# Moving output stores and residual rows from SyncE's DMA queue to GpSimd's in the second half of a quantized feed-forward

## Chip, cores and metric

One core of a Trainium2 chip runs the whole kernel in one launch. The metric is the device time of an execution in microseconds (us). The engines are TensorE (PE: matmuls; its weight loads are PEld), VectorE (DVE), ScalarE (ACT), GpSimd (POOL) and SyncE (SP). SP does no arithmetic: it issues DMAs. POOL can issue DMAs too.

## What is computed

Two batches of 2048 tokens of width 512 pass through four residual steps: a cross attention, a block that works on 256 selected tokens of each batch, a second cross attention, and a feed-forward with quantized activations and ternary weights. Only the last matters here:

```python
def bit_linear(x, w):          # act_quant: 8-bit integers per token, weight_quant: -1, 0, 1
    return einsum('bsd,hd->bsh', act_quant(x), weight_quant(w))
h = bit_linear(layernorm(x), w1)              # 512 -> 2048
h = silu(depthwise_conv1d(h, conv_w, conv_b)) # three taps along the tokens
x = x + tanh(g_ffn[1]) * bit_linear(h, w2)    # 2048 -> 512
```

`act_quant` needs the largest magnitude over a token's 2048 inner values before any of them can be rounded, so the step falls into a first half (up to `silu`) and a second half (rounding, the product with `w2`, the residual).

## The kernel before

The 4096 tokens are 8 blocks (g = 0 to 7) of 512. A block's inner values lie as 16 groups of 128 channels by 512 tokens.

**First half, block by block** (`first_half` L1179, `convolved` L1154). For each of the 16 channel groups, four matmuls (L1159) fill a PSUM tile `ph`. VectorE scales it into `u` (L1169). Two columns at the left of `u` come from `carry`, the last two tokens of the block before, copied by POOL (L1168), and POOL saves the new last two columns (L1170). ScalarE and VectorE apply the three taps (L1171, L1175). Four groups at a time go through Silu (L1200), are stored to DRAM as `h_d` (L1206), and then are overwritten in place by their magnitudes (L1207), so that instruction waits for the store. For the last block (g = LAST = 7) nothing is stored; the values stay in SBUF. The convolution makes a row tile begin one token before its block, so the first row tile of each batch has 127 rows, and each batch's very last token is left over for `last_tokens`.

**Rounding.** Blocks 0 to 3 (EARLY) are rounded to integers while the second attention still runs, and wait in DRAM as `hq_d`. Blocks 4 to 7 are rounded in the second half itself by `quantize_hidden` (L1334): it loads an inner row group from `h_d` into a pool of eight buffers, six ahead (L1355), multiplies by the scale on VectorE (L1364) and rounds on VectorE (L1370) or ScalarE (L1367, L1368). Blocks 0 to 3 are loaded ready-made (L1348).

**Second half** (the loop at L1430). For each of a block's four row tiles of 128 tokens, `down_and_out` (L1384) runs 16 matmuls of the integers with `w2q` (L1388) into one of four PSUM tiles, VectorE scales and adds the residual row tile (L1391), and the result is stored to the output (L1392). `row_tile` (L1311) loads the residual rows (L1318, L1320) about four row tiles ahead, into eight `x5` buffers (and two `x5w` buffers for the first two), so that a load waits for the store that last used its buffer. `last_tokens` (L1394) handles the two leftover tokens: Silu, largest magnitude, two transposes, scale, rounding, then two one-row `down_and_out` calls of 16 matmuls each. It is called whole ahead of block 6.

**What sets the order.** The functions are generators advanced by hand, which interleaves the blocks' steps with the attention and with each other. The layer that records them arranges each engine's instructions by its own estimate of their times. After that each engine works strictly in its order. A DMA-issuing instruction waits in its engine's order until the data and the buffer are free, and all that stands behind it on that engine waits too. In the program before, all DMAs of this stage are issued on SP: integers, inner-row stores and loads, residual rows and output stores, mixed.

Of the kernel before, what the change touches and what calls it, by code (L numbers as in the profile page):

```python
# [17 lines left out]
P = 128  # L18
# [3 lines left out]
BLK = 512  # L22
TB = BLK // P
NBLK = S // BLK
# [19 lines left out]
def flamingo_kernel(ctx: ExitStack, tc: tile.TileContext, a: dict, out: bass.AP):  # L44
    nc = tc.nc
# [699 lines left out]
    with ExitStack() as st:  # L745
# [16 lines left out]
            out=pick,  # L762
            in_=pick,
# [10 lines left out]
            out=after,  # L774
            in_=after,
# [310 lines left out]
    LAST = B * NBLK - 1  # L1086
    EARLY = 4
    hq_d = [dramp.tile([P, HC, BLK], BF16, name=f"hq_d{g}") for g in range(EARLY)]
    x3_d = [dramp.tile([S, D], F32, name=f"x3_d{b}") for b in range(B)]
# [64 lines left out]
    def convolved(g, c, z):  # L1154

        cr = carry[g // NBLK]
        ph = ps_mm.tile([P, BLK], F32, name="ph", tag="mm")
        for d in range(DC):
            nc.tensor.matmul(  # L1159
                ph,  # L1160
                w1q[:, d, ts(c, P)],
                xiT[g][:, d, :],
                start=(d == 0),
                stop=(d == DC - 1),
            )

        u = act4.tile([P, BLK + 2], F32, name="u", tag="u", bufs=3)
        nc.gpsimd.tensor_copy(u[:, 0:2], cr[:, c, :])  # L1168
        nc.vector.tensor_tensor(u[:, 2:], ph, inv_b[g], ALU.mult)  # L1169
        nc.gpsimd.tensor_copy(cr[:, c, :], u[:, BLK:])  # L1170
        nc.scalar.activation(  # L1171
            z, u[:, 1 : BLK + 1], AF.Identity, scale=cw[:, c, 1:2], bias=cb[:, c : c + 1]
        )
        for k in (0, 2):
            nc.vector.scalar_tensor_tensor(  # L1175
                z, u[:, ds(k, BLK)], cw[:, c, k : k + 1], z, ALU.mult, ALU.add
            )
# [96 lines left out]
    def beside4(u, share=2):  # L1274


        for _ in range(share):
            advance(ending)
            advance(stream)
        if u is None or u % 4 != 1:  # L1280
            advance(later)
# [29 lines left out]
    def row_tile(g, i):  # L1311

        t = w5[0].tile([P, D], F32, name="x5w", tag="x5w", bufs=2)
        if g * TB + i > 1:
            t = act5[0].tile([P, D], F32, name="x5", tag="x5", bufs=8)
        r, p = g % NBLK * BLK + i * P - 1, 0
        if r < 0:
            nc.sync.dma_start(out=t[0:1, :], in_=x3_d[g // NBLK][0:1, :])  # L1318
            r, p = 0, 1
        nc.sync.dma_start(out=t[p:, :], in_=x3_d[g // NBLK][ds(r, P - p), :])  # L1320
        return t, r, p

    def second_half_starts():
        units.close()
        w5.append(s4.enter_context(tc.tile_pool(name="w5", bufs=1)))
        w5.append(w5[0].tile([P, HC, D], BF16, name="w2q"))
        nc.sync.dma_start(out=w5[1], in_=w2_d)
        ps_5.append(psum_pool(s4, "s5_o", 4))
        quantizing.extend(quantize_hidden(g) for g in range(2))
        for q in quantizing:  # L1330
            next(q, None)
        ahead.extend(row_tile(0, i) for i in range(2))

    def quantize_hidden(g):  # L1334

        hq[g] = []

        def integer_tile():

            pool, bufs = (w5[0], 12) if next(next_integers) % 24 < 12 else (act5[0], 12)  # L1340
            hq[g].append(pool.tile([P, GQ, BLK], BF16, name="hq", tag="hq", bufs=bufs))
            return hq[g][-1]

        if g < EARLY:
            for k in range(HC // GQ):
                if g == 1 and k == HC // GQ // 2:
                    yield
                nc.sync.dma_start(out=integer_tile(), in_=hq_d[g][:, ts(k, GQ), :])  # L1348
            return

        def load(c):
            if g == LAST:
                return kept[c // GC][:, c % GC, :]
            h = xr.tile([P, D], F32, name="x3", tag="x3")
            nc.sync.dma_start(out=h, in_=h_d[g][:, c, :])  # L1355
            return h

        AHEAD = 6
        hs = [load(c) for c in range(AHEAD)]
        s_b = scales_spread(g)  # L1360
        yield
        for c in range(HC):
            h = hs.pop(0)
            nc.vector.tensor_tensor(h, h, s_b, ALU.mult)  # L1364
            q = (integer_tile() if c % GQ == 0 else hq[g][-1])[:, c % GQ, :]
            if c % 4:
                nc.scalar.activation(h, h, AF.Copy, bias=RND)  # L1367
                nc.scalar.activation(q, h, AF.Copy, bias=-RND)  # L1368
            else:
                nc.vector.tensor_scalar(q, h, RND, RND, ALU.add, ALU.subtract)  # L1370
            if c + AHEAD < HC:
                hs.append(load(c + AHEAD))
            if c % 2:
                yield
# [6 lines left out]
    act5.append(s4.enter_context(tc.tile_pool(name="act5", bufs=1)))  # L1381
    w2q = w5[1]

    def down_and_out(rows, col, n, t, to, p=0):  # L1384

        po = ps_5[0].tile([n, D], F32, name="po4", tag="o4")
        for c in range(HC):
            nc.tensor.matmul(  # L1388
                po, rows(c), w2q[:, c, :], start=(c == 0), stop=(c == HC - 1)
            )  # L1390
        nc.vector.scalar_tensor_tensor(t, po, col, t, ALU.mult, ALU.add)  # L1391
        nc.sync.dma_start(out=to, in_=t[p:, :])  # L1392

    def last_tokens():  # L1394

        h = act5[0].tile([P, B, HC], F32, name="hl", tag="hl")
        nc.scalar.activation(h, z_last, AF.Silu)
        own = row4.tile([P, B], F32, name="ownl", tag="lm")
        nc.vector.tensor_reduce(own, h, AX.X, ALU.max, apply_absolute_value=True)
        pm = ps_mm.tile([P, B, P], F32, name="pml", tag="mm")  # L1400
        for b in range(B):
            nc.tensor.transpose(pm[:, b, :], own[:, b : b + 1].to_broadcast([P, P]), ident)
        m = row4.tile([P, B], F32, name="ml", tag="lm")
        nc.vector.tensor_reduce(m, pm, AX.X, ALU.max)
        nc.vector.tensor_scalar(m, m, 1e-5, None, ALU.max)
        s = row4.tile([P, B], F32, name="sl", tag="ls")
        nc.vector.reciprocal(s, m)
        nc.vector.tensor_scalar(s, s, 127.0, None, ALU.mult)
        fin = row4.tile([P, B], F32, name="fl", tag="lf")
        nc.vector.reciprocal(fin, s)  # L1410
        nc.vector.tensor_scalar(fin, fin, finstep, None, ALU.mult)
        q = act5[0].tile([P, B, HC], BF16, name="ql", tag="ql")
        for b in range(B):
            nc.vector.tensor_scalar(h[:, b, :], h[:, b, :], s[:, b : b + 1], None, ALU.mult)
        nc.vector.tensor_scalar(q, h, RND, RND, ALU.add, ALU.subtract)
        for b in range(B):
            t = act5[0].tile([P, D], F32, name="x5", tag="x5", bufs=8)[0:1, :]
            nc.sync.dma_start(out=t, in_=x3_d[b][S - 1 : S, :])
            down_and_out(
                lambda c: q[:, b, c : c + 1],  # L1420
                fin[0:1, b : b + 1],
                1,
                t,
                out[(b + 1) * S - 1 : (b + 1) * S, :],
            )

    while later:
        advance(later)
    ahead.extend(row_tile(0, i) for i in range(2, TB))
    for g in range(LAST + 1):  # L1430
        if g == LAST - 1:
            while stream or ending:
                beside4(None)
            last_tokens()
        behind = quantizing[1] if g == 0 else quantize_hidden(g + 1) if g < LAST else iter(())
        for i in range(TB):
            t, r, p = ahead.pop(0)
            down_and_out(
                lambda c: hq[g][c // GQ][:, c % GQ, ts(i, P)],
                hid_f[:, g * TB + i : g * TB + i + 1],  # L1440
                P,
                t,
                out[ds(g // NBLK * S + r, P - p), :],
                p,
            )
            if g < LAST:
                ahead.append(row_tile(g + 1, i))
            for _ in range(3):
                next(behind, None)
                beside4(None, 1)  # L1450
# [65 lines left out]
```

## Time and profile before

| what | value |
|---|---|
| median of 3 runs | 1788.83 us (1788.56 to 1795.08) |
| the profiled execution, its own time | 1791.24 us |
| its span | 1789.2 us |
| mean granted TensorE clock | 0.966 |
| PE busy | 1647.3 us (92% of the span) |
| DVE busy | 1250.1 us (70%) |
| ACT busy | 1101.7 us (62%) |
| POOL busy | 536.0 us (30%) |
| hardware DMA queue of SP | 192.23 MB, 31.5% of 16 engines |
| GpSimd's software DMA queue | 2.10 MB, 0.6% |
| last attention block's projections end | about 1616 us |

Times inside the profile are us from the start of the span. "Granted clock" is the share of full speed that TensorE was given in a stretch. A wait row reads "who waited, at which line <- who ended it: total us, times, longest us". A timeline row gives start, duration, engine, line, operation and tiles; SPq rows are DMA issues on SP, and their duration is the time of the issue, not of the transfer. Digits of names are left out, so the tile `x` stands for `x3` and `x5` alike: `x<-h_d` is a load of inner rows (L1355), `x<-x_d` a load of residual rows, `out_x<-x` an output store.

### The profile page before, as it was taken

The page shows a single profiled execution, that of the slowest core. Times are in us where ns is not written, and L with a number is a line of the kernel's source. Part 1 is how long each engine was busy: PE and PEld are TensorE (multiplying, and loading weights), DVE is VectorE, ACT ScalarE, POOL GpSimd, SP SyncE. Part 2 cuts the span into 40 slices and gives each one's busy share as a digit, 9 for nine tenths or more (in the row PEclk, how much of TensorE's full clock was granted, in tenths as well). Part 3 has the DMA queues.
Part 4 walks back from the last instruction along what each step waited for, and adds up shares of the span by engine and source line. Part 5 has one row for each costly group of instructions (what it writes and reads, how often), then busy time and mean ns, then how long its engine had stood idle before and what let it go on. Part 6 is the DMA issues. An engine that isn't in the chain of part 4 may idle for free.

```text
span 1789.2 us, 25277 instructions
## 1 busy us (share of the span) xinstructions
PE 1647.3 (92%) x8122; PEld 864.8 (48%) x8122; DVE 1250.1 (70%) x2544; ACT 1101.7 (62%) x3170; POOL 536.0 (30%) x671
## 2 busy tenths in 40 slices
PE   6999889899999889999999999999999999889968
PEld 3544444455555665755444544445454544434423
DVE  4566878865767443344378789897998789686956
ACT  2876566456553233345367778787787778744555
POOL 2534443342440011033134242432424224231100
PEclk9999999999999999999999999999999999899979
DMA  6011011121007861630012333233242233157374
GB/s 215 7 66 55 35 60 66 59 65 54 25 36 250 287 190 64 190 83 25 19 53 95 127 122 117 91 130 110 94 167 76 87 105 130 62 210 249 123 233 173
DMA packets 119828, 196.99 MB, mean 110 GB/s; under 512 B 12900, under 2 KB 50532, under 8 KB 115984
## 3 DMA queue, kind: packets, MB, share of 16 engines
q1 hardware_dynamic: 117872, 192.23, 31.5%
q0 software_dynamic: 960, 2.10, 0.6%
q8 instruction: 64, 1.05, 0.2%
q10 hardware_dynamic: 864, 1.05, 0.2%
q14 instruction: 68, 0.56, 0.1%
HBM read 120.89 MB, written 74.45 MB: 109 GB/s over the span
## 4 chain that ended last, share of the span: by engine, by line
PE 29%; DVE 15%; DMA 5%; ACT 4%; issue 2%; POOL 1%; SPq 1%; DVEq 0%; POOLq 0%; ACTq 0%
PE pq L253 8%; PE pp L320 8%; DVE h L1175 4%; PE po L302 3%; PE ph L1159 3%; PE sc L276 3%; PE po L1388 2%; PE tp L294 2%; DMA x<-h_d 1%; DVE u L1169 1%; DVE AT L295 1%; DVE nmx L119 1%; DMA hq<-hq_d 1%; DVE hf L1258 1%; DMA h_d<-h 1%
## 5 line engine op out<-in xcount | busy, mean ns | idle before, releaser
L122 ACT ACTIVATE A<-sc,nmx 128x128 f32<-128x128 f32 x1024 | 363.8, 385 | 131.5 <-DVE nmx L119 121.7
L131 POOL TENSOR_TENSOR A<-A,rden 128x512 f32<-128x512 f32 x256 | 275.9, 1079 | 506.7 <-DVE rden L130 410.8
L320 PE MATMUL pp<-L_wo,OT 128*128 128x512 f32 x768 | 366.8, 609 | 18.0 <-DVE x L329 11.9
L253 PE MATMUL pq<-xnT,L_wq 128*128 128x512 f32 x768 | 345.7, 598 | 12.2 <-DVE x L329 12.2
L122 ACT ACTIVATION_READ_ACCUMULATOR A<-sc,nmx 128x1 f32 x1024 | 229.7, 224 | 0.0
L253 PEld LDWEIGHTS pq<-xnT,L_wq 128*128 128x128 f32 x768 | 142.8, 191 | 172.1 <-issue 151.3
L119 DVE TENSOR_REDUCE nmx<-sc 128x4 f32<-128x512 f32 x256 | 168.6, 678 | 71.8 <-PE sc L276 71.6
L320 PEld LDWEIGHTS pp<-L_wo,OT 128*128 128x128 f32 x768 | 136.5, 193 | 164.4 <-issue 133.2
L1175 DVE SCALAR_TENSOR_TENSOR h<-u,cw,h 128x512 f32<-128x512 f32 x256 | 205.0, 834 | 6.0 <-ACT h L1171 5.5
L294 PE MATMUL tp<-ident,A 128*128 128x128 f32 x1024 | 164.4, 284 | 18.7 <-POOL A L131 13.2
L294 PEld LDWEIGHTS tp<-ident,A 128*128 128x128 f32 x1024 | 118.4, 143 | 87.6 <-issue 41.9
L295 DVE COPY AT<-tp 128x512 f32<-128x512 f32 x192 | 129.8, 678 | 43.5 <-PE tp L294 42.8
L276 PEld LDWEIGHTS sc<-L_kT,qT 32*128 32x128 f32 (+1 forms) x2048 | 110.6, 192 | 71.0 <-issue 58.5
L1388 PE MATMUL po<-w2q,hq 128*128 128x512 bf16 x512 | 122.2, 394 | 20.0 <-DVE hq L1370 9.0
L276 PE MATMUL sc<-L_kT,qT 32*128 32x128 f32 (+1 forms) x2048 | 137.0, 293 | 3.8 <-ACT A L122 3.2
L1171 ACT ACTIVATE h<-u,cb,cw 128x512 f32<-128x512 f32 x128 | 99.1, 808 | 64.7 <-DVE u L1169 53.6
L302 PE MATMUL po<-AT,L_v 128*32 128x512 f32 (+1 forms) x512 | 119.3, 657 | 11.7 <-DVE AT L295 11.1
L1159 PE MATMUL ph<-xiT,w1q 128*128 128x512 bf16 x512 | 124.3, 379 | 1.9 <-DVE u L1169 1.5
L1169 DVE TENSOR_TENSOR u<-ph,inv_b 128x512 f32<-128x512 f32 x128 | 84.9, 682 | 31.4 <-PE ph L1159 27.3
L130 DVE RECIPROCAL rden<-den 128x4 f32<-128x4 f32 x256 | 43.3, 169 | 80.0 <-ACT A L122 72.8
L1168 POOL COPY u<-carry 128x2 f32<-128x2 f32 x128 | 48.7, 382 | 167.3 <-DVE h L1175 141.3
L1170 POOL COPY carry<-u 128x2 f32<-128x2 f32 x128 | 49.8, 394 | 150.9 <-DVE u L1169 149.1
(238 smaller groups left out, 2362.6 us busy)
## 6 DMA issues: line engine op xcount, KB each, us to landing
h_d<-h SPq DMA_DIRECT2D x28, 1024.0 KB, 4.1
x_d<-x SPq DMA_DIRECT2D x64, 256.0 KB, 3.1
hf<-h_d SPq DMA_DIRECT2D x64, 256.0 KB, 3.4
x<-x_d SPq DMA_DIRECT2D x61, 256.0 KB, 4.7
x<-h_d SPq DMA_DIRECT2D x48, 256.0 KB, 5.5
x_d<-xo SPq DMA_DIRECT2D x32, 256.0 KB, 2.1
xf<-x_d SPq DMA_DIRECT2D x32, 256.0 KB, 3.6
hq_d<-hi SPq DMA_DIRECT2D x64, 128.0 KB, 1.8
```

Source lines behind the costliest of these rows:

```text
L119: nc.vector.tensor_reduce(nmx, sc, AX.X, ALU.max, negate=True)
L122: nc.scalar.activation(out_tile[:, h, :], sc[:, h, :], AF.Exp, bias=nmx[:, h : h + 1], accum_out=den[:, h : h + 1],)
L131: nc.gpsimd.tensor_tensor(out_tile, out_tile, rden.unsqueeze(2).to_broadcast([P, n, width]), ALU.mult,)
L253: nc.tensor.matmul(pq, W.wq[:, d, ts(e, P)], xnT[:, d, :], start=(d == 0), stop=(d == DC - 1),)
L276: nc.tensor.matmul(sc[h][:, t, :], qT[e % cpg][r, ts(t, P)], W.kT[r, b, e, :], start=True, stop=True,)
L294: nc.tensor.transpose(tp[:, t, :], A[:, t, :], ident)
L295: copy(AT, tp.rearrange("p t n -> p (t n)"))
L302: nc.tensor.matmul(po[h * dh : (h + 1) * dh, :], W.v[:, b, ts(hd, dh)], AT[c * hpc + h], start=True, stop=True,)
L320: nc.tensor.matmul(pp, OT[e][:, ts(i, P)], W.wo[:, e, :], start=(e == 0), stop=(e == nE - 1),)
L1159: nc.tensor.matmul(ph, w1q[:, d, ts(c, P)], xiT[g][:, d, :], start=(d == 0), stop=(d == DC - 1),)
L1175: nc.vector.scalar_tensor_tensor(z, u[:, ds(k, BLK)], cw[:, c, k : k + 1], z, ALU.mult, ALU.add)
L1388: nc.tensor.matmul(po, rows(c), w2q[:, c, :], start=(c == 0), stop=(c == HC - 1))
```

## The change

In the second half, residual-row loads (L1318, L1320) and output stores (L1392) are issued on GpSimd's queue; only block 7's output stores stay on SP. Block 7's carry copies (L1168, L1170) go from GpSimd to VectorE. `last_tokens` becomes a generator that is advanced once after each row tile of blocks 6 and 7, so that its transposes, its scale and rounding, and its two products come after row tiles 0, 1 and 3 of block 6; the products then stand between blocks 6 and 7. Its own residual loads stay on SP, its output stores go to GpSimd's queue.

```diff
-        nc.gpsimd.tensor_copy(u[:, 0:2], cr[:, c, :])
+        carried = nc.vector if g == LAST else nc.gpsimd
+        carried.tensor_copy(u[:, 0:2], cr[:, c, :])
         nc.vector.tensor_tensor(u[:, 2:], ph, inv_b[g], ALU.mult)
-        nc.gpsimd.tensor_copy(cr[:, c, :], u[:, BLK:])
+        carried.tensor_copy(cr[:, c, :], u[:, BLK:])
...
         if r < 0:
-            nc.sync.dma_start(out=t[0:1, :], in_=x3_d[g // NBLK][0:1, :])
+            nc.gpsimd.dma_start(out=t[0:1, :], in_=x3_d[g // NBLK][0:1, :])
             r, p = 0, 1
-        nc.sync.dma_start(out=t[p:, :], in_=x3_d[g // NBLK][ds(r, P - p), :])
+        nc.gpsimd.dma_start(out=t[p:, :], in_=x3_d[g // NBLK][ds(r, P - p), :])
...
-    def down_and_out(rows, col, n, t, to, p=0):
+    def down_and_out(rows, col, n, t, to, p=0, queue=nc.gpsimd):
...
-        nc.sync.dma_start(out=to, in_=t[p:, :])
+        queue.dma_start(out=to, in_=t[p:, :])
...
             nc.tensor.transpose(pm[:, b, :], own[:, b : b + 1].to_broadcast([P, P]), ident)
+        yield
...
         nc.vector.tensor_scalar(q, h, RND, RND, ALU.add, ALU.subtract)
+        yield
+        yield
         for b in range(B):
...
-            last_tokens()
+            last = last_tokens()
...
                 p,
+                nc.sync if g == LAST else nc.gpsimd,
             )
             if g < LAST:
                 ahead.append(row_tile(g + 1, i))
+            if g >= LAST - 1:
+                next(last, None)
```

## The prediction

> **What bounds the kernel now.** I first read the page's 40 slices. TensorE (PE) is busy in nearly all of them, and its dips come late, where the granted clock (PEclk) dips too. The change touches only the last stage, so I cut the end into stretches by what TensorE works on and read the engines' busy time in each:
>
> ```profile
> core 0: us, PE busy (x) PEld busy (x) DVE busy (x) ACT busy (x) POOL busy (x), PEclk, DMA share, GB/s
> 1569.00:1600.00 31.00, 29.71 (x89) 12.96 (x90) 29.26 (x40) 15.19 (x15) 15.86 (x27) 1.00 0.75 267
> 1600.00:1616.00 16.00, 9.97 (x22) 4.15 (x20) 10.53 (x17) 7.73 (x6) 1.43 (x4) 0.79 0.22 90
> 1616.00:1643.00 27.00, 22.97 (x108) 10.95 (x107) 13.62 (x28) 11.99 (x15) 1.20 (x2) 0.87 0.71 230
> 1643.00:1696.00 53.00, 51.63 (x244) 23.76 (x243) 49.01 (x82) 27.37 (x27) 12.13 (x29) 1.00 0.49 176
> 1696.00:1760.00 64.00, 46.77 (x195) 18.89 (x193) 42.23 (x83) 39.82 (x72) 0.00 (x0) 0.84 0.74 247
> 1760.00:1789.00 29.00, 24.77 (x111) 10.23 (x111) 17.91 (x30) 15.80 (x29) 0.00 (x0) 1.00 0.31 110
> ```
>
> TensorE stands still for 6.0 us in 1600–1616 (call it A), 4.0 in 1616–1643 (B), 1.4 in 1643–1696 (C), 17.2 in 1696–1760 (D) and 4.2 in the tail (E). A, B and D also run at a clock of 0.79 to 0.87. In C TensorE and VectorE (DVE) are both nearly full: block 7's first half and the down projections of blocks 0 to 3. Next, who waits for whom after 1600:
>
> ```profile
> DVE x L1364 <- DMA x<-h_d: 16.5, 7, 9.2
> ACT h L1207 <- DMA h_d<-h: 13.2, 3, 7.9
> PE po L1388 <- DVE hq L1370: 9.0, 2, 8.7
> ```
>
> Columns: total us, times, longest. Transfers end all three. The 7.9 us wait for an inner-row store is A (PE waits 6.03 us behind it), the 9.2 for an inner-row load is most of D. Why are they late? SyncE's (SP) own queue in D:
>
> ```profile
> 1719.05 0.26 SPq L1392 DMA_DIRECT2D out_x<-x  x1
> 1719.40 5.46 SPq L1355 DMA_DIRECT2D x<-h_d  x2
> 1724.95 0.53 SPq L1392 DMA_DIRECT2D out_x<-x  x1
> 1725.57 9.70 SPq L1355 DMA_DIRECT2D x<-h_d  x6
> ```
>
> An issue on SP normally takes 0.34 us. The store at 1719.05 is the 127-row one of block 4 (batch 1's first row tile). The two loads behind it take 5.46 us to issue, the next six 9.70, and that store lands 9.5 us after issue where the median is 2.0. The other 127-row transfers show the same: 1586.4 (the issue behind it 5.05 us), 1620.43 (7.88 us for two) and 1679.88 (lands after 12.3). Each inner-row transfer queued behind one is late: A follows 1586.4, B 1620.43, D 1719.05. And SP is held by what it waits for:
>
> ```profile
> SPq L1392 <- DVE x L1391: 42.6, 20, 8.0
> SPq L1320 <- DMA out_x<-x: 22.2, 12, 6.2
> ```
>
> The output stores wait for VectorE and the residual loads (buffers shared with those stores) for stores to land: 65 us in which the inner-row loads behind them can't go.
>
> **The change, part by part.** The profiled execution took 1791.24 us (span 1789.2, 2 us around it); the median of the runs is 1788.83, so I sum against 1791.24 and take 2.4 off.
>
> *Moved off SP:* 28 row-tile stores, 2 last-token stores and 34 residual-row DMAs, 64 issues, all four 127-row ones among them; on SP stay the 48 inner loads, block 7's four stores and the last tokens' two loads. In the changed program's order block 6's second inner store follows the 0.3 us integer loads directly, and each inner load waits only for its own buffer.
>
> *Stretch A.* In before the store could go when Silu ended at 1588.64, was issued at 1591.51 behind the 5.05 us, and landed at 1603.5. Alone it takes 4.1 us (the row `h_d<-h`), so about 1594; ScalarE (ACT) has other work to 1595.6. That removes 7.9 us of wait, TensorE's 6.0, and the half-speed matmuls after it (4 of 0.85 us in place of 0.43: 1.7). Against it: GpSimd (POOL) now issues three loads just ahead of the four bias adds (1571.48 in before) and the copies behind them. No POOL row shows this DMA; the nearest, the gather of 128 rows of 2 KB, takes 1.0 us (L970), the tiny one 0.6 (L66), the scatter 1.6 (L675). 3 x 1.0 = 3 us of delay to a copy that ScalarE waits for, perhaps 2 of it on the path (0 to 4.8). Sum: -7.7 + 2.2, so **-5.5**.
>
> *Stretch B.* The third inner store lands 7.9 us after issue with the 127-row store beside it; at 4.1 the fourth normalised tile, queued behind it on ACT, comes 3 us sooner. TensorE's transposes of the last block sit behind matmuls that wait for integer loads until 1636.93 (the 7.88 us issue); with loads early, the stretch from 1634.2 to the first matmul at 1642.3 shrinks from 8.1 us to about 4. POOL's rsqrt (L90) now stands behind four loads, 4 us from the moment the last projection ends, where statistics take 2 to 3 us anyway: cost 0 to 2, hidden mostly. Sum **-7**, at best -9, at worst -3.
>
> *Stretch C.* 32 carry copies move from POOL to VectorE, which is full (49.0 of 53). The nearest DVE rows:
>
> ```profile
> 1684.39 0.18 DVE L1219 TENSOR_TENSOR tap<-carry,cw 128x16 f32<-128x16 f32 x1
> 1684.49 0.17 DVE L1220 TENSOR_TENSOR z_last<-carry,cw 128x16 f32<-128x16 f32 x1
> ```
>
> Starts lie 0.10 us apart: 32 x 0.10 = 3.2 us; by duration 0.17 x 32 = 5.4. The handoff to POOL goes away (up to 2 back, and a gain of 1 isn't excluded). I take **+3** (-1 to +5.4).
>
> *Stretch D.* Now the loads start when the first buffers come free (1698–1699), not at 1703.24, and the 9.2 us hole behind 1719.05 closes. What is late next? The transfers themselves: 64 us x 247 GB/s = 15.8 MB. The best rates that this trace holds over 30 us and more are 267 (first row above) and 287 (page). At 280 the stretch needs 56 us, at 267 59, at 287 55. VectorE's 42, ACT's 40 and TensorE's 47 (about 40 at full clock) fit below that. So -8; the clock returns with the hole, **-9** in all (-4 to -17, the last if TensorE's idle went entirely).
>
> *Stretch E.* The last tokens' 32 matmuls (7.07 us at 1748.58) filled a hole; now they stand between blocks 6 and 7, where block 7's integers take VectorE and ACT 14 us after block 6's anyway while TensorE has some 20 matmuls left (4 us): 4 + 7 < 14, **0** (0 to +5 if those integers are early). Last stores stay on SP: 2.0 us to land.
>
> Sum: -5.5 - 7 + 3 - 9 = -18.5; 1791.2 - 18.5 - 2.4 = **1770**.
>
> **Two rules against the rows.** For 127 rows: the Trainium skill, "DMA: Bandwidth & Descriptors", section on why a DMA increments its semaphore by 16, says that a hardware-queue DMA over 127 partitions runs on one engine, and that GpSimd's queue spread 127 over all 16. The rows agree with the first half (9.5 us for 254 KB, 2.0 for 256); no run here shows the second. If it is false, the queued transfers still share that one engine, and A, B and D give half. Against the change speaks "SBUF — State Buffer", "Two separate sides", with its trap: GpSimd can't write descriptors while VectorE runs a two-port operation; a DMA of 620 ns became 3100. The gathers here took 0.95 to 1.09 us beside VectorE at work. At 1.0 us POOL needs 2 us per row tile for its store and load, plus up to 3.4 us where a load waits for the store before it; a row tile comes every 4.7 to 5 us on average. That fits. At 3.1 it would not. I take 1.0, since VectorE's stretches of such operations here are short (L1370, 0.42 us).
>
> **Rivals.**
> 1. *GpSimd's queue becomes the bound (slower).* About eight store-and-load pairs in a row each contain a landing wait (3.4 us at best for a gather). At 2.5 us per issue a pair takes 8.4 us: eight are 67 us where 55 are there, 12 late; then 20 tiles at 2 x 2.5 + 1.5 against 5.2 lose 26 more. 38 - 18.5 = +19: 1808. It decides from about 1.9 us per issue (2 x 1.9 + 1.5 = 5.3). For it: the rule, and the 1.6 us scatter. Against: 1.0 us gathers, and residual rows asked for eight tiles ahead.
> 2. *One engine keeps the 127 rows, or the transfers in D don't speed up:* A -2, B -3, C +3, D -4: about 1783.
> 3. *Copies at POOL's price* (0.39 each, L1170): C +12.5, sum -9: 1780.
> 4. *TensorE full:* idle of A, B and D (27) and half of their clock loss (4), less C's 3: -28, 1760.
>
> **How the numbers follow.** Forecast 0.45 (1763 to 1778), rival 4 0.17, rivals 2 and 3 together 0.22, rival 1 0.16 (some of it mild). About 0.5% (9 us) is what a measurement of this kernel can tell. Under 1780: 0.45 + 0.17 + 0.06 = 0.68. Within: 0.18. Slower: 0.14. Range 1756 to 1793.
>
> **What would show it.** A: the in-place magnitude (L1207 here) waits under 1 us for `h_d<-h`. B: no SP issue above 2 us near the block-0 stores. C: copies at 0.1 us pitch on DVE. D: DMA above 265 GB/s in its stretch, waits for `x<-h_d` under 8 us in total. POOL: its DMA issues near 1.0 us, 127-row ones landing in under 5. I am wrong if those issues take 2 us or more, or if the loads in D are no faster though nothing stands before them.

## The result and the profile after

The changed kernel took 1768.99 us (median of 4 runs, 1767.29 to 1771.65) beside 1788.69 before: ratio 0.9887, 95% interval 0.9863 to 0.9911. Taken once more later, beside other experiments, it gave 0.9908 (0.9892 to 0.9923). So it is about 1% faster; 1770 was predicted. The profiled execution took 1771.65 us, its span 1770.0.

The same stretches as before, by what TensorE works on; columns are time, then PE, PEld, DVE, ACT and POOL busy, granted clock, DMA share, GB/s:

```profile
1573.00:1604.00 31.00, 28.79 (x85) 12.53 (x88) 30.49 (x41) 18.55 (x17) 15.88 (x28) 1.00 0.77 271
1604.00:1614.00 10.00, 10.00 (x30) 4.29 (x29) 10.00 (x16) 4.79 (x5) 1.90 (x4) 1.00 0.33 134
1614.00:1637.00 23.00, 19.16 (x102) 9.37 (x103) 13.79 (x35) 11.89 (x16) 8.12 (x14) 1.00 0.96 355
1637.00:1688.00 51.00, 50.01 (x228) 22.71 (x232) 49.88 (x110) 26.59 (x25) 11.42 (x21) 1.00 0.44 150
1688.00:1739.00 51.00, 42.76 (x190) 17.22 (x193) 41.99 (x84) 40.85 (x74) 10.23 (x18) 1.00 0.89 305
1739.00:1770.00 31.00, 26.67 (x120) 10.94 (x120) 18.38 (x31) 14.74 (x27) 4.93 (x9) 0.98 0.28 100
```

A no longer has TensorE standing still (10.00 busy of 10.00), its clock is back at 1.00, and D fell to 51 us at 305 GB/s. The waits in the changed part after 1590:

```profile
POOL x L1321 <- DMA out_x<-x: 58.0, 17, 6.7
POOL out_x L1393 <- DVE x L1392: 33.0, 10, 7.1
...
DVE x L1365 <- DMA x<-h_d: 5.3, 6, 1.4
...
ACT h L1208 <- DMA h_d<-h: 3.5, 1, 3.5
```

The waits for stores and for VectorE now stand on POOL. The wait for inner-row loads fell from 16.5 us to 5.3, that of the in-place magnitude from 13.2 to 3.5. The four 127-row transfers, now on GpSimd's queue (last column: us from issue to landing):

```profile
x5w<-x_d POOLq DMA_DIRECT2D x1, 254.0 KB, 8.6
out_x<-x5w POOLq DMA_DIRECT2D x1, 254.0 KB, 8.1
x<-x_d POOLq DMA_DIRECT2D x1, 254.0 KB, 2.8
out_x<-x POOLq DMA_DIRECT2D x1, 254.0 KB, 4.2
```

Their 128-row neighbours on the same queue take 9.0, 8.7, 4.6 (the median of the loads) and 3.9: the 127 rows are no longer special. A GpSimd issue takes 0.55 us (0.50 to 0.78).

To compare kernels I use the end of the last product of attention weights with values (L302), just ahead of the first changed instruction, and these marks behind it: end of the last attention projection (A), first matmul of block 7's first half (B), end of the reduce that gives block 7's scale (C), end of block 6's last scaling on VectorE (D), end of the span (E). The part ahead of them is the same work in every kernel (VectorE, ScalarE and GpSimd run the same instructions there in the same order in all profiles), yet its end lay between 1569.0 and 1576.7 us. So medians that lie 3 or 4 us apart tell little here. The sum of the stretches, which leaves that part out, is the better measure, though it comes from one profile of each kernel; the changed kernel's two profiles differ by 2 us in it.

| kernel | median us | ratio (95% interval) | A | B | C | D | E | sum |
|---|---|---|---|---|---|---|---|---|
| before | 1788.7 | 1 | 47.4 | 25.9 | 53.7 | 63.9 | 29.4 | 220 |
| changed | 1769.0 | 0.9887 (0.9863-0.9911) | 41.0 | 20.7 | 53.6 | 50.4 | 31.3 | 197 |
| e11 changed again | 1774.9 | 0.9908 (0.9892-0.9923) | 41.0 | 22.4 | 53.6 | 50.1 | 32.2 | 199 |
| e1 before, 127 rows on GpSimd's queue | 1765.9 | 0.9874 (0.9858-0.9890) | 40.7 | 17.5 | 54.4 | 46.7 | 30.5 | 190 |
| e2 before, 127 cut 112 + 15 on SP | 1762.6 | 0.9858 (0.9839-0.9877) | 39.2 | 18.0 | 53.8 | 48.5 | 29.8 | 189 |
| e3 changed, 127 rows back on SP | 1804.0 | 1.0073 (1.0055-1.0091) | 50.7 | 32.3 | 54.5 | 58.6 | 32.4 | 229 |
| e4 changed, carry on GpSimd | 1775.2 | 0.9924 (0.9908-0.9940) | 41.0 | 22.5 | 53.8 | 49.4 | 32.2 | 199 |
| e5 e1 + carry on VectorE | 1762.5 | 0.9842 (0.9820-0.9864) | 40.7 | 17.5 | 53.6 | 47.2 | 30.5 | 190 |
| e6 e1 + last tokens in pieces | 1767.2 | 0.9871 (0.9849-0.9893) | 40.7 | 17.5 | 54.3 | 46.4 | 31.2 | 190 |
| e7 changed, 128-row stores on SP | 1771.8 | 0.9893 (0.9866-0.9919) | 41.0 | 22.4 | 53.6 | 47.3 | 32.5 | 197 |
| e8 changed, 128-row loads on SP | 1765.3 | 0.9865 (0.9844-0.9885) | 41.4 | 18.0 | 54.3 | 46.9 | 32.3 | 193 |
| e9 before, 127 cut 122 + 5 on SP | 1768.4 | 0.9890 (0.9869-0.9910) | 39.2 | 18.8 | 53.8 | 53.7 | 29.6 | 195 |
| e10 e2 + carry on VectorE | 1764.4 | 0.9838 (0.9818-0.9859) | 39.2 | 18.0 | 53.6 | 49.1 | 30.1 | 190 |

### The profile page after: what moved, and what is told of

It is laid out like the page before. It is cut to its first block, busy times and chain, and to the rows that moved or that the text cites. A ratio compares the mean times of both kernels' runs of the same rounds, so it can differ in the third digit from the quotient of the medians.

```text
span 1770.0 us, 25204 instructions
## 1 busy us (share of the span) xinstructions
PE 1642.2 (93%) x8076; PEld 863.0 (49%) x8122; DVE 1251.5 (71%) x2576; ACT 1101.4 (62%) x3170; POOL 556.4 (31%) x703
## 4 chain that ended last, share of the span: by engine, by line
PE 28%; DVE 18%; ACT 4%; DMA 3%; issue 2%; POOL 1%; SPq 0%; DVEq 0%; POOLq 0%; ACTq 0%
PE pq L253 8%; PE pp L320 7%; DVE h L1176 5%; PE po L302 3%; PE sc L276 3%; PE ph L1159 3%; PE tp L294 2%; DVE u L1170 2%; DVE nmx L119 1%; PE po L1389 1%; DVE AT L295 1%; DMA hf<-h_d 1%; DVE hf L1259 1%; ACT A L122 1%; DVE h L1209 1%
## 5 line engine op out<-in xcount | busy, mean ns | idle before, releaser
L302 PE MATMUL po<-AT,L_v 128*32 128x512 f32 (+1 forms) x512 | 121.6, 667 | 11.5 <-DVE AT L295 11.0
L1389 PE MATMUL po<-w2q,hq 128*128 128x512 bf16 x501 | 116.6, 380 | 9.3 <-ACT hq L1369 5.1
L1170 DVE TENSOR_TENSOR u<-ph,inv_b 128x512 f32<-128x512 f32 x128 | 85.4, 683 | 32.4 <-PE ph L1159 28.3
L1169 POOL COPY u<-carry 128x2 f32<-128x2 f32 x112 | 42.8, 384 | 147.0 <-DVE h L1176 121.8
L1159 PEld LDWEIGHTS <-w1q 128*128 128x128 bf16 x512 | 49.2, 98 | 81.2 <-issue 37.6
```

The lines of the kernel that those rows point to most:

```text
L302: nc.tensor.matmul(po[h * dh : (h + 1) * dh, :], W.v[:, b, ts(hd, dh)], AT[c * hpc + h], start=True, stop=True,)
L1159: nc.tensor.matmul(ph, w1q[:, d, ts(c, P)], xiT[g][:, d, :], start=(d == 0), stop=(d == DC - 1),)
L1389: nc.tensor.matmul(po, rows(c), w2q[:, c, :], start=(c == 0), stop=(c == HC - 1))
```

## The experiments

My theory after the result had two causes: the 127-row transfers block SP's queue, and SP waits for VectorE and for landing stores while inner-row loads stand behind. The rivals: only the first, or only the second.

**e1: the kernel before, with only the four 127-row transfers moved.**

```diff
-        nc.sync.dma_start(out=t[p:, :], in_=x3_d[g // NBLK][ds(r, P - p), :])
+        (nc.gpsimd if p else nc.sync).dma_start(
+            out=t[p:, :], in_=x3_d[g // NBLK][ds(r, P - p), :]
+        )
...
-        nc.sync.dma_start(out=to, in_=t[p:, :])
+        (nc.gpsimd if p else nc.sync).dma_start(out=to, in_=t[p:, :])
```

> The kernel before, with only the four 127-row transfers (two residual loads, two output stores) moved to GpSimd's queue; all 128-row ones, the carry copies and the last tokens as before. Theory (both causes count: a 127-row transfer blocks SyncE's queue, and SyncE waits for VectorE and for landing stores with inner-row loads behind it): the holes of A, B and D that start at a 127-row transfer close, so A -6, B -4, D -7 (the inner loads still start some 5 us late and run at about 270 GB/s), 17 us less than before: about 1772. If the 127-row transfers are all of it: 1766 to 1769, with D as fast as in the changed kernel (51 us). If the waits on SyncE are what counts: above 1783.

Four moved transfers out of 64 take 30.5 us off the stretches, more than the whole change (23.2). By the ratio, too, e1 is at least as fast as the changed kernel (0.9874 beside 0.9887 and 0.9908). The time fell below the figure that my theory gave, and to the edge of the range of the rival "only the 127 rows". What SP waited for after 1590, in e1:

```profile
SPq L1394 <- DVE x L1393: 50.6, 26, 8.1
SPq L1320 <- DMA out_x<-x: 15.0, 12, 2.4
```

That is 65.6 us, where the kernel before had 42.6 + 22.2 = 64.8. The waits are all still there, and D is the shortest of all but one kernel (e6). So the second half of my theory falls: in e1 these waits cost nothing that shows. And D's rows in e1:

```profile
1683.00:1730.00 47.00, 43.41 (x197) 17.17 (x194) 42.39 (x84) 39.63 (x71) 0.53 (x1) 1.00 0.89 304
```

**e2: the kernel before, each 127-row transfer cut into 112 and 15 rows, all on SP.**

```diff
-        nc.sync.dma_start(out=t[p:, :], in_=x3_d[g // NBLK][ds(r, P - p), :])
+        for lo, hi in ((1, 113), (113, P)) if p else ((0, P),):
+            nc.sync.dma_start(
+                out=t[lo:hi, :], in_=x3_d[g // NBLK][ds(r + lo - p, hi - lo), :]
+            )
```

The output store is cut in the same way.

> The kernel before, with each of the four 127-row transfers cut into 112 rows and 15 rows, all still on SyncE's queue. If the queue is blocked because a transfer of 127 rows sits on one engine, 112 rows go like 128 and 15 rows hold a single engine for an eighth of the time at most: the issues of 5 to 10 us behind them vanish, and the time is that of the run that moves them to GpSimd, within 4 us (about 1773). If what matters is that these transfers leave SyncE's queue, or that batch starts are slow for another reason, nothing changes: about 1788.

As expected, and a little better: 189 us over the stretches. Around the store of block 4's first row tile, which the prediction shows at 1719.05 for the kernel before, SP's issues are now:

```profile
1700.23 0.34 SPq L1396 DMA_DIRECT2D out_x<-x  x1
1700.62 0.43 SPq L1397 DMA_DIRECT2D out_x<-x  x1
1701.14 0.88 SPq L1358 DMA_DIRECT2D x<-h_d  x2
```

The two loads behind it take 0.88 us to issue, where it was 5.46. So it isn't the queue that matters, but the shape: the same bytes on the same queue, in two issues instead of one. The SBUF side of the 112-row piece begins at partition 1 like that of the 127 rows, so an odd start isn't the cause either.

**e9: a dose between, 122 and 5 rows.** The edit is e2's, with 123 in the place of 113.

> The kernel before, with each of the four 127-row transfers cut into 122 rows and 5 rows, all on SyncE's queue (the cut into 112 and 15 gave 1762.6 us). A dose between: the Trainium skill, 'DMA: Bandwidth & Descriptors', section on why a DMA increments its semaphore by 16, says that such a transfer uses as many engines as the largest divisor up to 16 of its row count, which is 2 for 122, 16 for 112 and 1 for 127. On two engines at the 25 to 29 GB/s that one shows in the kernel before, 244 KB take about 4.7 us where 9.5 were taken: half of each hole stays, A 43 to 44, B 20 to 22, D 52 to 56, and the time is 1773 to 1778. If only the count 127 is special (or any cut helps): 1763. If a hole doesn't shrink with more engines but needs all 16: 1785 to 1789.

The rule holds where it can be read directly. What the core's DMA engines moved around the 127-row load, in the kernel before from 1583 to 1604 us (40 slices of 0.53 us; upper line busy tenths, lower GB/s):

```profile
DMA  9999999999971000098999998961000000000000
GB/s 371 394 418 394 418 390 320 269 297 414 402 300 66 27 23 27 27 109 242 496 406 417 429 402 347 414 254 39 27 23 27 23 27 35 16 31 31 20 23 27
```

Around the store of block 4's first row tile, cut at 122 rows (e9, 1700 to 1716 us):

```profile
DMA  9999998789999999989979521111279992277997
GB/s 333 384 328 348 359 266 241 292 338 323 374 343 348 333 333 318 312 307 374 353 277 343 220 92 51 51 51 51 92 189 338 343 394 97 82 195 220 343 394 282
```

And the same place cut at 112 rows (e2, 1700 to 1716 us):

```profile
GB/s 348 348 297 348 338 394 405 400 399 359 353 358 394 410 353 348 333 374 405 312 318 292 251 225 302 343 394 358 374 333 307 353 353 353 348 353 384 394 323 225
```

In the kernel before, the rate falls twice to some 25 GB/s: everything else is done, and one engine works alone. With 122 rows the floor is 51, twice that: two engines. With 112 there is no floor. The busy share of the 16 DMA engines, next to last in these rows (the kernel before, then e9), says the same, 0.06 for one of 16 and 0.13 for two:

```profile
1598.00:1603.00 5.00, 3.30 (x10) 1.15 (x8) 0.60 (x1) 0.00 (x0) 0.76 (x2) 1.00 0.06 26
1709.60:1711.20 1.60, 0.00 (x0) 0.00 (x0) 0.00 (x0) 0.00 (x0) 0.00 (x0) 1.00 0.13 51
```

The second hole of the first view (1597 to 1604) is the end of the inner-row store of A: it keeps one engine's rate, as if that engine's share of the store had queued behind the 127 rows. This is read from rates and shares; the trace doesn't name the engines. My size for the time was too high (1768 in place of 1773 to 1778): A and B stand at or near e2's times (39.2 and 18.8) in spite of the shorter hole, only D shows it, 5.2 us above e2.

**e3: the changed kernel, with only the 127-row transfers back on SP.** The edit is e1's in the changed kernel, the other way round.

> The changed kernel, with only the four 127-row transfers back on SyncE's queue. Theory (both causes): A (the load blocks the first inner store) comes back with 6 us, B with about 3, D with about 6 since the inner loads queued behind the store of block 4's first row tile are held for its 9 us but start earlier than before: 1769 + 15 = about 1784. If only the waits on SyncE count: within 3 us of the changed kernel. If only the 127-row transfers count: 1788, as before.

None of the three: 1804, slower than the kernel before by 0.73% (0.55 to 0.91). SP's issues in e3 (start, duration of the issue, engine, line, operation, tiles):

```profile
1626.90 0.51 SPq L1395 DMA_DIRECT2D out_x<-x5w  x1
1627.46 30.23 SPq L1351 DMA_DIRECT2D hq<-hq_d  x18
...
1731.30 0.26 SPq L1395 DMA_DIRECT2D out_x<-x  x1
1731.65 33.35 SPq L1358 DMA_DIRECT2D x<-h_d  x24
```

In e3 SP has little left but loads, so what queues directly behind a 127-row store is what TensorE and VectorE need next: A took 50.7 us, B 32.3, and in B TensorE waited 9.2 us for a single integer load. That the store also waits for VectorE ahead of these loads is part of it; the two weren't told apart. Over the stretches the four transfers on SP cost 29 to 32 us here (229 against 199 and 197), and 30 in the kernel before (220 against 190 in e1). So a queue of its own for the loads doesn't make a blocking transfer in it cheaper, and e3 pays for the 60 other moves besides.

**e4 and e5: the carry copies alone.** e4 is the changed kernel with `carried = nc.gpsimd`, e5 is e1 with the copies on VectorE for the last block.

> The changed kernel, with the 32 carry copies of the last block back on GpSimd. The stretch that holds them (C) took 53.0 us in both kernels, so the copies on VectorE (32 x 0.07 = 2.2 us) and the handoff to GpSimd that they save would balance: within 2 us of the changed kernel, 1767 to 1771. If the copies on VectorE cost what I predicted (+3), the time falls to 1766. If GpSimd, which now issues stores and loads (0.55 us each), delays the copies and with them VectorE's and ScalarE's work, it rises by up to 15 us (16 channels x 1 us).

> The kernel before, with the four 127-row transfers on GpSimd's queue (1765.9 us) and, new, the last block's 32 carry copies on VectorE. GpSimd issues only four transfers here. Theory: the copies matter only where GpSimd is held by transfers that it issues (putting them back on GpSimd cost the changed kernel 6 us), so here nothing moves: 1764 to 1768. If the copies on VectorE save the handoff in any setting: about 1760. If they cost VectorE what I predicted (+3): 1769.

By medians e4 lost 6 us and e5 gained 3. By stretches neither moved: C is 53.8 in e4 against 53.6, and 53.6 in e5 against 54.4 (the 53.0 of the expectation counts to the start of the reduce). The changed kernel taken again showed why the medians mislead:

> The changed kernel once more, beside the other two on the same chip: 1767 to 1772 as before. It tells what of the differences of 3 to 6 us between runs of different sessions is the session: if its median lies at 1773 or more, the 6 us that the carry copies on GpSimd seemed to cost the changed kernel shrink to within the spread; and its second profile shows whether B (20.7 us) and D (50.4) repeat.

It gave 1774.9 us, e4's time, and its L302 mark lay at 1574.6 against 1572.9. So the 6 us lie within the spread of one kernel. By C, the copies cost or bring at most 1 us.

**e6: e1 with the last tokens in pieces** (the change's `last_tokens` and its loop).

> The kernel before, with the four 127-row transfers on GpSimd's queue (1765.9 us) and, new, the last tokens in pieces, as in the changed kernel. Theory: their 32 matmuls (7 us) leave stretch D, where transfers set the pace and TensorE has 4 us to spare, and go to the tail, where the stretch grew by 1.9 us in the changed kernel: within 2 us, 1764 to 1768, rather up than down. If the pieces are a gain by themselves (D shorter by up to 7 us and the tail by nothing): 1759. If the tail takes them in full: 1770 and more.

D 46.4 against 46.7, E 31.2 against 30.5: nothing that can be told from zero.

**e7 and e8: which of the moved 128-row transfers costs.** e7 is the changed kernel with `(nc.gpsimd if p else nc.sync)` for the output stores, e8 with the same for the residual loads.

> The changed kernel, with the 128-row output stores back on SyncE's queue; the 127-row ones and all residual loads stay on GpSimd's. Theory: what the changed kernel loses against the run that moves only the 127-row transfers (B 3.2 us, D 3.7) comes from SyncE issuing its loads with nothing in between: 18 integer loads in 20 us then run beside the third inner store (8.1 us to land). With the stores in SyncE's queue these loads are spaced out by the waits for VectorE: B 18, D 48, about 1763. If the residual loads on GpSimd (five at once, just as the third inner store goes) are what delays it: as the changed kernel, 1769. If the waits on SyncE for VectorE cost after all: above 1772.

> The changed kernel, with the 128-row residual loads back on SyncE's queue; the 127-row ones and all output stores stay on GpSimd's. SyncE then waits for stores to land that GpSimd issues (3.5 us to land, where SyncE's own take 2.0). If the residual loads beside the third inner store are what costs B its 3.2 us: B 18 and 1764 to 1766. If SyncE's burst of integer loads is: B as in the changed kernel, 20 to 21, and 1769. If waits for landing stores ahead of the inner loads are dear: D above 54 and the time above 1773.

In B the first idea, SyncE's unbroken burst of integer loads, falls: with the stores back on SP (e7) the burst is broken up and B is still 22.4. With the loads back on SP (e8) B is 18.0. ScalarE's waits in B, for the changed kernel:

```profile
ACT h L1208 <- DMA h_d<-h: 3.5, 1, 3.5
```

The same row in e7:

```profile
ACT h L1208 <- DMA h_d<-h: 3.6, 1, 3.6
```

In e8 and in e1 there is no such row. In the changed kernel GpSimd issues eight residual loads between 1614.2 and 1620.3 (0.55 us each), and block 6's fourth inner-row store goes at 1615.39 beside them and lands after 8.1 us (under 6 in e1 and e8). On SP's queue most of these loads come behind that store. So the moved residual loads give back some 3 to 5 us in B.

In D the changed kernel and its repeat took 50.4 and 50.1 us and e4, which has both moves too, 49.4; e7 took 47.3, e8 46.9, e1 46.7. Either move alone is free, both together cost about 3 us. More traffic doesn't explain it. What the DMA engines moved in D, in the changed kernel and then in e7:

```profile
DMA packets 7230, 15.34 MB, mean 304 GB/s; under 512 B 934, under 2 KB 934, under 8 KB 7226
DMA packets 7815, 15.54 MB, mean 328 GB/s; under 512 B 958, under 2 KB 958, under 8 KB 7812
```

Beside e1, which moved 14.20 MB at 305 GB/s, the 1.14 MB more of the changed kernel would make up the 3.7 us. But e7 moved more than either, at a higher rate, in 3 us less than the changed kernel. Why the rate stays lower with both moves is open.

**e10: the two edits that lost nothing, together** (e2 and the carry copies on VectorE).

> The kernel before, with the four 127-row transfers cut into 112 and 15 rows on SyncE's queue, and the last block's carry copies on VectorE: the two edits that lost nothing so far, and no transfer moved to GpSimd. Expected 1759 to 1763, below the changed kernel (1769) with intervals apart. If the 3.4 us by which the carry copies on VectorE lowered the median beside four GpSimd transfers were chance: 1763. If the cut only works as well as the move to GpSimd: 1766.

1764.4 us, ratio 0.9838 (0.9818 to 0.9859), against 0.9908 (0.9892 to 0.9923) of the changed kernel taken beside it: it is faster than both kernels. It isn't better than e2 (190 and 189 over the stretches); the cut is all of it.

## Why the prediction was right, and where its steps were off

The time, 1770, was right, and the main mechanism too: a 127-row transfer on the hardware queue runs on one engine and holds what follows. But that the sum hit was in part luck: errors cancelled. A to D gave 25.2 us where I had 18.5, E took back 1.9, and 3.9 more lay ahead of the first changed instruction, where nothing had changed.

- **Moved off SP.** The step "65 us in which the inner-row loads behind them can't go" failed as a cost. In e1 65.6 us of such waits remain and the gain is larger. The late start of the inner-row loads in D (1703.24) goes with the 127-row transfers as well. SP's waits for stores to land, in the kernel before (1676 to 1705) and in e1 (1664 to 1700):

```profile
SPq L1320 <- DMA out_x<-x: 14.4, 6, 6.2
SPq L1320 <- DMA out_x<-x: 4.9, 5, 2.1
```

The wait of 6.2 us stands behind the 127-row load at 1679.88. In e1 the loads start 2 us after block 7's scale, not 7.
- **A**, -5.5 predicted, -6.4 measured. The gain is about as worked out. GpSimd's three issues took 0.60 to 0.65 us, not 1.0, so the +2.2 was too much.
- **B**, -7 predicted, -5.2 measured. The step that failed is the landing of block 6's fourth inner store (the prediction's "third"), 4.1 assumed, 8.1 measured: ScalarE's wait for it grew from 2.7 us to 3.5 instead of going away. In the kernel before that store was issued at 1619.07, ahead of the 127-row one and not behind it as I had read. With only the 127-row transfers moved B gives -8.4 (e1). I charged GpSimd for issuing the residual loads, but gave no price to their transfers.
- **C**, +3 predicted, -0.1 measured. On VectorE the 32 copies start about 0.07 us apart, 2.2 us in all, and the handoff to GpSimd that they save seems to give this back (C alone shows it).
- **D**, -9 predicted, -13.5 measured. The term "at 280 the stretch needs 56 us" was the wrong one: the best rate of the trace before was no limit; the stretch at 267 held one-engine holes itself. Without such holes the engines keep 304 to 328 GB/s over all of D (the changed kernel, e1, e7). In e1 D is -17.2, which was the far end of my span.
- **E**, 0 predicted, +1.9 measured (2.8 in the repeat). The last tokens' 32 matmuls (7 us) now run in E (from 1744.6), where they stood in D before; other matmuls left E, so that TensorE is busy 26.67 us there, 24.77 before. I had taken them to fit into idle time of TensorE. The pieces alone measured +0.7 (e6), so most of it isn't told apart from spread.

Of the signs to look for, one failed: two of the four 127-row transfers landed after 8.6 and 8.1 us, not in under 5, as late as their 128-row neighbours.

Rival 1 (GpSimd bound) is excluded: 0.55 us an issue against the 1.9 from which it decides. (Residual rows are asked for four row tiles ahead, not eight.) The trap that I had weighed, from the Trainium skill, "SBUF — State Buffer", "Two separate sides" (GpSimd can't write descriptors beside two-port VectorE work), shows at most in small. Of the 25 GpSimd issues in D and E, 22 took at most 0.56 us; the other three (0.69 to 0.78) are those in which a rounding on VectorE (L1371) began 0.15 to 0.24 us after the issue did. One of them:

```profile
1700.66 0.76 POOL L1393 DMA_DIRECT2D out_x<-x  x1 [7.08 <-DVE x L1392]
1700.88 0.42 DVE L1371 TENSOR_SCALAR hq<-x 128x512 bf16<-128x512 f32 x1
```

The repeat has two such issues (0.74 and 0.76), again the longest in D and E. No edit tested this cause. Rival 2's premise, one engine on GpSimd's queue as well, is excluded by the landings: at 25 GB/s one engine needs some 10 us for 254 KB, and two of them took 2.8 and 4.2. Rival 3 is excluded by e4 and e5. Rival 4 came near: TensorE is busy 50.01 of 51 us in C, but 42.76 of 51 in D. (Its clock term of 4 comes to about 6 by the busy times and clocks of its rows.)

I left out a rule on the same page as the one I used. The Trainium skill, "DMA: Bandwidth & Descriptors", section "Issuing engines are not separate DMA queues", says that transfers share the same engines whoever issues them, and that spreading the issue only saves issuing time. By it, taken at its word, 60 of the 64 moved transfers bring nothing. That is what e1 shows, and B and D show them costing about 7 us (8 in the repeat).

## What to carry to other kernels

Look at the row count of every DMA before asking which queue it should be on: in the timeline of issues, a duration of several us where others take 0.34, and next to it a stretch at one sixteenth of the DMA rate, mean a transfer that runs on one engine. Cut it into a piece whose row count is a multiple of 16 and a small rest (112 and 15 here), on the queue where it is. A queue that waits a lot isn't a cost until an experiment that leaves these waits in place fails to be as fast.

## What the runs showed of the hardware that was not expected

- The floor of the DMA rate counts the engines: about 25 GB/s for 127 rows, 51 for 122, none below 225 for 112, as e9 expected from the row-count rule.
- GpSimd's queue spreads 127 rows: 2.8 to 8.6 us to landing, like 128 rows beside them.
- Output stores of 256 KB landed after 3.5 us (median) on GpSimd's queue, and after 2.0 to 2.7 (medians) on SP's, where the traces give only 2 to 10 landings each. Other traffic differed too.
- Every GpSimd issue above 0.6 us in D and E had a rounding on VectorE begin within it.
- The same work ahead of the change ended up to 7.7 us apart from profile to profile, more than most edits here moved.
